# Attention and a depthwise convolution on one core: whole-array products gathered into one stretch per image

## The chip, the cores and the metric

The kernel runs on one core of a Trainium2 chip. The metric is the device time of one execution in microseconds (us). Three runs of the kernel before took 2955.26, 2948.74 and 2949.14 us, median 2949.14. One execution was also profiled; it was timed at 2951.07 us, and the span from its first to its last instruction is 2949.3 us. PE is the matrix engine, DVE the vector engine, ACT the scalar engine, POOL and SP the two engines whose queues issue most of the transfers (DMA).

## The reference

The input x is (16, 384, 32, 32) in float32: 16 images, 384 channels, 1024 pixels. Two layers follow each other, each a normalisation over 32 groups of channels, a branch, and the addition of the branch to its input:

```python
# layer 0: attention over the 1024 pixels, 8 heads of 48 channels
qkv = einsum('bnc,oc->bno', tokens(gn(x)), w_qkv)
attn = softmax(q @ k.T * 48 ** -0.5)
x = x + from_tokens(einsum('bnc,oc->bno', attn @ v, w_proj) + b_proj)
# layer 1: depthwise 7x7 convolution, the weight averaged over four rotations
x = x + dwconv(gn(x), w_sym, stride=1, pad=3)
```

The mean and variance of the first normalisation come from the input x, those of the second from the result of layer 0.

## The kernel before

**Tiles.** The 384 channels of an image are three tiles of 128 partitions by 1024 pixels, named by k (or o, for outputs). Heads are taken in four windows per image; a window has 16 key blocks of 64 keys, so an image has 64 steps (`PER_B`), and the kernel has 1024.

**Products on PE.** Two kinds alternate. The whole-array products use all 128 rows and columns of PE: q and k (`qk_step`, line 445, three pieces t = 0, 1, 2 of two products each; the fourth tile of q and k is gathered by six transfers in `qk_rest`, line 461), v (`v_step`, line 471, four products) and the projection (`proj_step`, line 597, three). The tiled products address PE as four tiles of 48 or 64 rows by 64 columns: the scores S of a step (`s_step`, line 516) and the product of their exponentials with v (`av_step`, line 536, called AV here). Each float32 product is two passes, so a step has 8 matmuls for S and 8 for AV.

**PSUM.** All whole-array products and all S share one pool of three buffers (tag "s"). ACT empties them: a copy of 128x1024 for each qk product (line 452), four small copies for each v product (line 491), the bias for a projection (line 605), and the exponential of an S into one of eight buffers (line 524).

**What else ACT does, in its one queue.** It normalises the next image's x (`x_apply`, three instructions at line 367, which wait for the load of x, line 164), squares the result of layer 0 for its variance (`x1_squares`, line 288), forms the factors of the second normalisation (`x1_groups`, lines 306 to 308, with two table loads), and applies them (`x1_chains`, line 367 again, which wait for the factors brought by the transfer at line 281).

**DVE.** It runs the convolution as taps (line 683): 49 per tile, 147 per image, in turn over the three tiles of one image, with the softmax work between them: reciprocals of the sums (line 566) and the divide (line 578), each of which waits for a small transfer on SP. Of the last two images some tiles and rows go to PE and ACT instead.

**What sets the order.** There is no scheduler at run time. The kernel is written out by a planner in Python (line 898 on), and the order of its instructions on each engine is fixed then; real time enters through the waits alone. The planner keeps two clocks, `clock` for PE and `vclock` for DVE, advanced by fixed costs (`US_STEP` and so on). `after(wait, cost, f)` puts work for DVE on a list with a due time; `catch_up(to)` writes out what is due, or taps, until `vclock` reaches `to`. Work for ACT goes into the list `applies`, in order, each with a due time and a cost; `act_slot(free)` writes out those that are due and cost no more than `free`. It is called between steps (with 4.3) and ahead of each qk product (with 9.0). A due time is thus a place in an engine's queue. If what it waits for is late, all that stands behind it in that queue waits too.

**Where the whole-array products stand.** `chunks` holds the three qk pieces of each image. `other` writes one out after every 8 steps if it is due: the pieces 0 and 1 of an image at 32 and 16 steps before the image begins, piece 2 at 16 steps into it. The v products follow the image's first 8 S. The projection of the former image follows when its last divide is done and 7 us have passed, between two steps. So an image breaks its steps five times. `scores` runs S ahead of AV by `LOOK` + 1 = 5 steps, across the border between two images. x has a single buffer: the next image is loaded (`begin_x`) once piece 2 is written.

Of the kernel before, what the change touches and what calls it, by code (L numbers as in the profile page):

```python
# [45 lines left out]
def kernel(  # L46
# [27 lines left out]
    B, C, H, W = x.shape  # L74
    N = H * W
    NK = C // P
    D = C // HEADS
    NP = HEADS // 2
    NT = N // P
# [32 lines left out]
    def run(general):  # L112
        tag = "g" if general else "f"
        with ExitStack() as stack:
# [25 lines left out]
            xds, shs, pss, mats, psums = {}, {}, {}, {}, {}  # L140
# [49 lines left out]
            v = wpool.tile([P, NT, VG] if general else [P, 2 * NT, VW], F32, name="v")  # L190
# [307 lines left out]
            def place(n):  # L498

                w, kb = divmod(n, 2 * NT)  # L500
                return w // NP, w % NP // 2, w % 2, kb
# [406 lines left out]

            US_STEP, US_QK, US_V, US_PROJ = 1.717, 5.3, 4.0, 5.3
            LOOK = 4
            clock, vclock, last_image, catching = 0.0, 0.0, 1e9, False
            later, count = [], 0
            chains, active = deque(), []
            NS = U * 2 * NT

            SIZES = [8] * 8
            PER_B = 2 * NT * NP

            def now():
                return vclock if catching else max(clock, vclock)
# [110 lines left out]
                catching = False  # L1033


            chunks, proj = deque(), deque()
            ready = {}
            x1_stats = {}
            pe_conv, pe_loads = deque(), deque(
# [6 lines left out]
            def issue(c):  # L1046
                nonlocal clock
                kind, b, i = c
                if kind == "qk":
                    act_slot(9.0)  # L1050
                    for s in range(2):
                        qk_step(b, i, s)
                        clock += US_QK
                        if s == 0:

                            catch_up(clock)
                            act_slot(9.0)
                    if i == NK - 1:
                        qk_rest(b)
                        if b + 1 < B:  # L1060
                            begin_x(b + 1)
                else:
                    v_step(b, i)
                    clock += US_V

# [5 lines left out]
            def project(b):  # L1071
                nonlocal clock
                for o in range(NK):
                    proj_step(b, o)
                    clock += US_PROJ
                    if b in ON_VECTOR:
                        after(8.0, 1.3, lambda o=o: x1_part(b, o))
                if b not in ON_VECTOR:
                    after(1.6, 0.2, lambda: x1_means(b))
# [15 lines left out]
            def x1_means(b):  # L1095
                st = x1_stats[b] = Stats(f"x1_{b}")
                st.bs = x1_bs[:, b % 2]
                nc.vector.scalar_tensor_tensor(
                    st.bs[:, :, 1::3],
                    psums.pop(b).unsqueeze(2).to_broadcast([P, NK, 2]),  # L1100
                    -1.0 / N,
                    x_mean[:, b, :].unsqueeze(2).to_broadcast([P, NK, 2]),
                    ALU.mult,
                    ALU.add,
                )
                applies.append((now() + 1.0, 4.2, lambda: x1_squares(b, st)))

            def x1_squares(b, st):
                for k in range(NK):
                    st.square(x1s[b, k], k)  # L1110
                st.gather_x1()
                after(11.0, 3.3 if b == B - 2 else 0.6, lambda: x1_aggregate(b, st))
# [9 lines left out]

            def x1_groups(b, st):
                st.groups_x1()
                applies.append((clock + 6.5, 3.7, lambda: x1_chains(b, st)))

            def act_slot(free, slow=1.0):
                nonlocal act_free
# [4 lines left out]
                    act_free = clock + slow * cost  # L1133
                    f()

            s_next, act_free = 0, 0.0

            def scores(to):

                nonlocal s_next, clock  # L1140
                while s_next < min(to, NS):
                    b, q, _, _ = place(s_next)
                    while chunks and chunks[0][1:] <= (b, q + 1):
                        issue(chunks.popleft())
                    s_step(s_next)
                    s_next += 1
                    clock += US_STEP / 2

            def between_steps():
                catch_up(clock)  # L1150
                if clock >= act_free:
                    act_slot(4.3, 2.3)
                if proj and proj[0][0] <= clock:
                    project(proj.popleft()[1])
                    catch_up(clock)

            def x1_chains(b, st):
                nonlocal vclock
# [38 lines left out]
            def begin_x(b):  # L1197
                load_x(b)
                if b == 1:
                    after(10.0, 3.8, lambda: x_channels(b))  # L1200
                else:
                    applies.append((now() + 7.0, 3.7, lambda: x_apply(b, None)))

            def x_channels(b):
                st = Stats(f"x_{b}")
# [38 lines left out]
                    proj.append((now() + 7.0, b))  # L1244


            for b in range(B):
                chunks.extend(("qk", b, t) for t in range(NK))


            ones = tpool.tile([P, N], F32, tag="t", name="ones_warm")[:, 0:HALF]
            nc.vector.memset(ones, 1.0)
            warm = psum("warm")
# [21 lines left out]
            conv_weights()  # L1275
            means_of(st.bs, x_mean[:, 0, :])
            ready[0] = 0.0
            issue(chunks.popleft())
            issue(chunks.popleft())
            every = [(b, k) for b in range(2, B) for k in range(NK)]  # L1280
            for n, bk in enumerate(every):
                after(2.0 * n, 0.0, lambda bk=bk: stream_in(*bk))
# [53 lines left out]
                    elif h == 1:  # L1336
                        after(6.0, 1.2, lambda: conv_on_pe_end(b, k))

            def other(done):

                catch_up(clock)
                if chunks:
                    _, cb, t = chunks[0]
                    when = PER_B * cb + (-32, -16, 16)[t]
                    if ready.get(cb, 1e9) <= clock and done >= when:
                        issue(chunks.popleft())
                catch_up(clock)

            def first_half(b):

# [49 lines left out]
            for b, n0, size in [  # L1400
                (b, b * PER_B + sum(SIZES[:g]), SIZES[g]) for b in range(B) for g in range(len(SIZES))
            ]:
                r = n0 - b * PER_B
                if n0 == NS - PER_B:
                    last_image = clock
                if r == 0:
                    scores(n0 + 2 * LOOK)
                    for i in range(NT // 2):
                        issue(("v", b, i))
                elif r % (2 * NT) == 0:  # L1410
                    scores(n0 + LOOK + 3)
                ending = b == B - 1 and r + size == PER_B
                if ending:
                    scores(NS)
                    catch_up(clock)
                    assert not invs and not waiting
                    first_half(b)
                    loads(1)
                for n in range(n0, n0 + size):
                    scores(n + LOOK + 1)  # L1420
                    av_step(n)
                    clock += US_STEP / 2
                    between_steps()
                w = n0 // (2 * NT)
                if (n0 + size) % (2 * NT) == 0:
                    take(w)
                    finish(w)
                if ending:
                    fast_finish(b)
                else:  # L1430
                    other(n0 + size)
                if b == B - 4 and r == 32:
                    after(0.0, 2.0, check_early)
                if b == 2 and r == 40:
                    conv_prepare()
                if b == B - 1:

                    if once("mat_0", r >= 16):
                        mat = flat2(xpool.tile([P, NK, N], F32, tag="x", name="mat_0"))
                        conv_matrices(0, mat)  # L1440
                        late["w3"] = mat[:, 2 * SH * KS * CH :][:, 0:C]
                    if once("w", r >= 32 and b - 1 in x1_stats):
                        nc.sync.dma_start(wp, w4[:, 0:NK])
                        nc.sync.dma_start(late["w3"], w4[:, NK])
                    if once("mat_1", r >= 24):
                        conv_matrices(1, flat2(qkpool.tile([P, 2, N], F32, tag="qk", name="mat_1")))
                    if once("ones", r >= 32):
                        t = opool.tile([P, N], F32, tag="o", name="masks_1")
                        nc.sync.dma_start(t, masks.rearrange("p b c -> p (b c)"))
                        late["masks"] = t.rearrange("p (b c) -> p b c", c=P)  # L1450
                if b == B - 1:
                    if r >= 32 and (b, 0) not in x1s and all(c[0] > b - 2 for c in active):
                        for k in range(NK):
                            x1s[b, k] = rpool.tile([P, N], F32, tag="x1", name=f"x1_{b}_{k}")
                            nc.gpsimd.dma_start(
                                x1s[b, k], x[b, k * P : (k + 1) * P].rearrange("p h w -> p (h w)")
                            )
                if b == B - 1 and r in (32, 40, 48):
                    loads(1)
# [66 lines left out]
```

## Time and profile before

| what | us |
|---|---|
| median of three runs | 2949.14 |
| profiled execution, its own time | 2951.07 |
| profiled execution, span | 2949.3 |
| PE busy | 2893.5 (98%) |
| DVE busy | 2571.6 (87%) |
| ACT busy | 1578.0 (54%) |
| POOL busy | 262.1 (9%) |
| last AV of image 0 / 1 / 2 / 3 / 4 | 204.8 / 378.4 / 555.9 / 732.5 / 911.1 |
| last AV of image 14 / 15 | 2684.6 / 2850.8 |
| last matmul ends | 2934.6 |

A busy time is the union of an engine's instructions. Matmuls are pipelined and overlap in the records, so PE's share is near 100% even where their starts are further apart than they need be; for PE the distance from start to start is read. In a timeline the first number is the start, the second the length of a run of alike instructions, xN their number, and a bracket the idle time ahead and what ended it. The lines of an image repeat nearly alike from image to image.

### The profile page before, as it was taken

The numbers are of one execution on the slowest core, as the hardware profiler recorded it, in microseconds if no ns is written. First come the engines' busy times: TensorE is split into PE (matmuls) and PEld (weight loads), VectorE is DVE, ScalarE is ACT, GpSimd is POOL, SyncE is SP. The second block draws the span as 40 slices with busy tenths as digits, with TensorE's granted clock in tenths as the row PEclk, the third lists the DMA queues.
The fourth block names the chain that finished last, engine by engine and source line by source line (L and its number), as shares of the span: only waits on it lengthen the run. The fifth ranks groups of instructions, "written<-read, shape, count | busy, mean of one in ns | idle before, by whom it ended". The sixth has DMA issues, their size and how long they took to land. (4 is left out here: it accounts for less than half of the span.)

```text
span 2949.3 us, 46854 instructions
## 1 busy us (share of the span) xinstructions
PE 2893.5 (98%) x19638; PEld 1132.1 (38%) x19638; DVE 2571.6 (87%) x2562; ACT 1578.0 (54%) x1873; POOL 262.1 (9%) x411
## 2 busy tenths in 40 slices
PE   9999999999999999999999999999999999999998
PEld 4333343433434343343433434343343433434333
DVE  5412998989899898998999899898998999899989
ACT  3546555465555655455465555655455465554731
POOL 2211002110100101000010100101000010100201
PEclk9999999999999999999999999999999999999999
DMA  6433012130312203012130302203012030312447
GB/s 254 150 33 64 19 33 76 25 80 19 75 27 42 69 20 85 18 33 69 27 78 19 85 18 42 70 21 83 19 33 69 21 84 18 66 37 40 97 104 178
DMA packets 77485, 176.86 MB, mean 60 GB/s; under 512 B 32096, under 2 KB 34032, under 8 KB 75728
## 3 DMA queue, kind: packets, MB, share of 16 engines
q0 software_dynamic: 34336, 114.90, 15.9%
q1 hardware_dynamic: 41216, 55.21, 7.9%
q10 hardware_dynamic: 1712, 3.67, 0.5%
q8 instruction: 156, 2.56, 0.4%
q14 instruction: 65, 0.53, 0.1%
HBM read 118.61 MB, written 28.72 MB: 50 GB/s over the span
## 5 line engine op out<-in xcount | busy, mean ns | idle before, releaser
L683 DVE SCALAR_TENSOR_TENSOR x<-xn,wsym,x 128x899 f32<-128x899 f32 (+9 forms) x2170 | 2362.9, 1164 | 45.2 <-ACT xn L367 41.5
L524 ACT ACTIVATE e<-ps_s 128x1024 f32<-128x1024 f32 x1024 | 1020.3, 1025 | 534.7 <-PE ps_s L516 531.5
L516 PE MATMUL ps_s<-qk 48*64 48x512 f32 x8192 | 1049.3, 594 | 34.8 <-ACT e L524 30.0
L536 PE MATMUL acc<-e,v 64*64 64x512 f32 x8192 | 1046.8, 593 | 0.0
L516 PEld LDWEIGHTS ps_s<-qk 48*64 48x64 f32 x8192 | 306.3, 133 | 627.0 <-issue 532.9
L536 PEld LDWEIGHTS acc<-e,v 64*64 64x64 f32 x8192 | 310.5, 133 | 576.4 <-issue 575.4
L445 PE MATMUL ps_qk<-x,wqk 128*128 128x512 f32 x1152 | 507.3, 597 | 0.0
L445 PEld LDWEIGHTS ps_qk<-x,wqk 128*128 128x128 f32 x1152 | 215.2, 190 | 291.0 <-issue 282.3
L452 ACT COPY qk<-ps_qk 128x1024 f32<-128x1024 f32 x96 | 96.9, 1009 | 307.9 <-PE ps_qk L445 307.9
L471 PE MATMUL ps_v<-wv,x 128*128 128x384 f32 x768 | 252.0, 488 | 0.0
L597 PE MATMUL ps_proj<-o,wp 128*128 128x512 f32 x540 | 235.8, 595 | 0.0
L612 POOL DMA_DIRECT2D x<-in_x x45 | 39.3, 874 | 1927.5 <-ACT x L605 1484.6
L491 ACT COPY v<-ps_v 64x384 f32<-64x384 f32 x256 | 121.4, 474 | 137.0 <-PE ps_v L471 134.8
L471 PEld LDWEIGHTS ps_v<-wv,x 128*128 128x128 f32 x768 | 144.6, 190 | 110.5 <-ACT e L524 13.0
L578 DVE TENSOR_TENSOR o<-o,inv 128x1024 f32<-128x1024 f32 x63 | 77.0, 1222 | 103.0 <-DMA inv<-inv 85.7
L605 ACT ACTIVATE x<-ps_proj,bp 128x1024 f32<-128x1024 f32 x45 | 50.1, 1114 | 211.5 <-PE ps_proj L597 211.5
L597 PEld LDWEIGHTS ps_proj<-o,wp 128*128 128x128 f32 x540 | 101.4, 190 | 134.2 <-issue 123.1
L566 DVE RECIPROCAL rec<-sums 128x16 f32<-128x16 f32 x63 | 15.6, 248 | 143.7 <-DMA sums<-sum 143.6
L549 ACT COPY o<-acc 128x512 f32<-128x512 f32 x128 | 68.0, 586 | 22.8 <-PE acc L536 22.8
L367 ACT ACTIVATE xn<-x,sc_x 128x1024 f32<-128x1024 f32 x47 | 54.9, 1231 | 30.4 <-DMA sc_x<-gr_x 23.2
L390 DVE BATCH_NORM_STATS2 bs_all<-xs 128x6 f32<-128x512 f32 x84 | 53.0, 682 | 17.9 <-DMA xs<-in_x 17.7
L367 ACT ACTIVATE x<-x,x_sc 128x1024 f32<-128x1024 f32 x42 | 51.8, 1240 | 30.7 <-DMA x<-in_x 30.1
(144 smaller groups left out, 626.2 us busy)
## 6 DMA issues: line engine op xcount, KB each, us to landing
x<-in_x POOLq DMA_DIRECT2D x90, 512.0 KB, 5.8
inv<-inv SPq DMA_DIRECT2D x126, 256.0 KB
out<-x POOLq DMA_DIRECT2D x45, 512.0 KB, 4.2
xs<-in_x POOLq DMA_DIRECT2D x42, 512.0 KB, 6.3
qk<-qk POOLq DMA_DIRECT2D x96, 128.0 KB, 6.0
o<-o SPq DMA_DIRECT2D x180, 32.0 KB
sh<-xd SPq DMA_DIRECT2D x32, 160.0 KB
x<-in_x SPq DMA_DIRECT2D x6, 512.0 KB
```

Of the source, the lines that this page charges most:

```text
L367: nc.scalar.activation(dst, src, AF.Identity, bias=self.sc[:, k, 1:2], scale=self.sc[:, k, 0:1],)
L445: nc.tensor.matmul(ps[:, h, :], lhsT=wqk[:, k, s, t, :], rhs=xns[b][:, k, h * HALF : (h + 1) * HALF], start=(k == 0), stop=(k == NK - 1),)
L452: nc.scalar.copy(halves(qks[u][:, s, :]), ps)
L471: nc.tensor.matmul(ps[:, j, 0:C], lhsT=xns[b][:, k, t * P : (t + 1) * P], rhs=wv[:, k, :], start=(k == 0), stop=(k == NK - 1),)
L491: nc.scalar.copy(dst[:, :, 0 : HEADS // 2 * (D + 1)].rearrange("p k (h d) -> p k h d", d=D + 1)[:, :, :, 0:D], src.rearrange("p k (h d) -> ...
L516: nc.tensor.matmul(ps[64 * c : 64 * c + 64, a, :], lhsT=qk[r, 1, 64 * kb : 64 * kb + 64], rhs=qk[r, 0, h * HALF : (h + 1) * HALF], start=True,
L524: nc.scalar.activation(es[n], ps, AF.Exp, scale=SCALE)
L536: nc.tensor.matmul(accs[a][64 * j : 64 * j + 64, :], lhsT=v[rows, kb, c : c + 64], rhs=e[rows, j, :], start=(kb == 0), stop=(kb == 2 * NT ...
L549: nc.scalar.copy(half_of(w)[:, a, :], accs.pop(a))
L578: nc.vector.tensor_tensor(o, o, invs.pop(u).rearrange("p (a n) -> p a n", a=2), ALU.mult)
L597: nc.tensor.matmul(ps[:, h, :], lhsT=wp[:, t, o * P : (o + 1) * P], rhs=os_[b, t // 2][:, t % 2, h * HALF : (h + 1) * HALF], start=(t == 0 ...
L683: nc.vector.scalar_tensor_tensor(acc, xn1s[b, k].rearrange("p (h w) -> p h w", w=W)[:, iy, ix], wsym[:, k, dy + PAD, dx + PAD : dx + PAD + 1],
```

## The change

`other` and the list `chunks` go. At the beginning of each image a new function, `whole_array`, writes out in one stretch the pieces 0 and 1 of qk, the four v products and piece 2, all of the image itself, and ahead of each of these items the projection of the former image, if its time has come. S can no longer run past the border of an image: `s_limit` holds it back until the stretch is written. Four S then stand ahead of the steps instead of eight. After the stretch, if the former image's projection is still not written, the PE clock is put forward to it.

Three due times in `applies` move: the squares after the means from 1 to 5 us, the normalisation of x after its load from 7 to 13, the application of the second factors from 6.5 to 9. ACT gets a slot ahead of each v product too, for work that costs at most 3.0. The planner's costs of whole-array products are lower by 0.12 to 0.14 us, and it goes through an image in 16 groups of 4 steps instead of 8 of 8; before the last group of the last image it writes the first half of that image's projection (`first_half`), which therefore moves from 8 to 4 steps ahead of the end.

```diff
-            US_STEP, US_QK, US_V, US_PROJ = 1.717, 5.3, 4.0, 5.3
+            US_STEP, US_QK, US_V, US_PROJ = 1.717, 5.16, 3.88, 5.16
...
-            SIZES = [8] * 8
+            SIZES = [4] * 16
...
                 else:
+                    act_slot(3.0)
                     v_step(b, i)
...
-                applies.append((now() + 1.0, 4.2, lambda: x1_squares(b, st)))
+                applies.append((now() + 5.0, 4.2, lambda: x1_squares(b, st)))
...
-                applies.append((clock + 6.5, 3.7, lambda: x1_chains(b, st)))
+                applies.append((clock + 9.0, 3.7, lambda: x1_chains(b, st)))
...
-                while s_next < min(to, NS):
-                    b, q, _, _ = place(s_next)
-                    while chunks and chunks[0][1:] <= (b, q + 1):
-                        issue(chunks.popleft())
+                while s_next < min(to, s_limit):
                     s_step(s_next)
...
                     act_slot(4.3, 2.3)
-                if proj and proj[0][0] <= clock:
-                    project(proj.popleft()[1])
-                    catch_up(clock)
...
-                    applies.append((now() + 7.0, 3.7, lambda: x_apply(b, None)))
+                    applies.append((now() + 13.0, 3.7, lambda: x_apply(b, None)))
...
-            for b in range(B):
-                chunks.extend(("qk", b, t) for t in range(NK))
...
-            def other(done):
-
-                catch_up(clock)
-                if chunks:
-                    _, cb, t = chunks[0]
-                    when = PER_B * cb + (-32, -16, 16)[t]
-                    if ready.get(cb, 1e9) <= clock and done >= when:
-                        issue(chunks.popleft())
-                catch_up(clock)
+            def whole_array(b):
+
+                nonlocal clock, s_limit
+                items = [("qk", 0), ("qk", 1), *(("v", i) for i in range(NT // 2)), ("qk", 2)]
+                for kind, i in items:
+                    if proj and proj[0][0] <= clock:
+                        project(proj.popleft()[1])
+                    issue((kind, b, i))
+                    catch_up(clock)
+                while b and ((b - 1) not in x1_stats and (b - 1) not in psums):
+                    clock = max(clock, proj[0][0] if proj else clock + 1.0)
+                    catch_up(clock)
+                    if proj and proj[0][0] <= clock:
+                        project(proj.popleft()[1])
+                s_limit = (b + 1) * PER_B
...
                 if r == 0:
-                    scores(n0 + 2 * LOOK)
-                    for i in range(NT // 2):
-                        issue(("v", b, i))
+                    whole_array(b)
+                    scores(n0 + LOOK)
...
-                    other(n0 + size)
+                    catch_up(clock)
```

More of the change, by code (lines that the diff above doesn't have):

```diff
@@ L1033, in catch_up @@
                 catching = False
-            chunks, proj = deque(), deque()
+            proj = deque()
             ready = {}
@@ L1134, in act_slot @@
                     f()
-            s_next, act_free = 0, 0.0
+            s_next, s_limit, act_free = 0, 0, 0.0
             def scores(to):
                 nonlocal s_next, clock
-                while s_next < min(to, NS):
-                    b, q, _, _ = place(s_next)
-                    while chunks and chunks[0][1:] <= (b, q + 1):
-                        issue(chunks.popleft())
+                while s_next < min(to, s_limit):
                     s_step(s_next)
@@ L1277, in run @@
             ready[0] = 0.0
-            issue(chunks.popleft())
-            issue(chunks.popleft())
             every = [(b, k) for b in range(2, B) for k in range(NK)]
@@ L1337, in conv_piece @@
                         after(6.0, 1.2, lambda: conv_on_pe_end(b, k))
-            def other(done):
-                catch_up(clock)
-                if chunks:
-                    _, cb, t = chunks[0]
-                    when = PER_B * cb + (-32, -16, 16)[t]
-                    if ready.get(cb, 1e9) <= clock and done >= when:
-                        issue(chunks.popleft())
-                catch_up(clock)
+            def whole_array(b):
[12 more added lines that the diff above has]
+                s_limit = (b + 1) * PER_B
             def first_half(b):
```

## The prediction

> **What bounds the kernel now.** I read the busy shares first, then the waits, then the timelines of one image (number 4, from 732.9 us on), then the end.
>
> ```profile
> PE 2893.5 (98%) x19638; PEld 1132.1 (38%) x19638; DVE 2571.6 (87%) x2562; ACT 1578.0 (54%) x1873; POOL 262.1 (9%) x411
> ```
> PE looks full, so it sets the time of all but the end, and a gain must come out of its spacing. Its timeline (start, length, engine, line, tiles):
>
> ```profile
> 791.20 1.04 PE L536 MATMUL acc<-e,v 64*64 64x512 f32 x8
> 792.17 10.57 PE L445 MATMUL ps_qk<-x,wqk 128*128 128x512 f32 x24
> 802.67 2.81 PE L516 MATMUL ps_s<-qk 48*64 48x512 f32 x24
> ...
> 815.62 1.04 PE L536 MATMUL acc<-e,v 64*64 64x512 f32 x8
> 819.61 1.82 PE L516 MATMUL ps_s<-qk 48*64 48x512 f32 x8 [2.95 <-ACT e L524]
> 821.18 1.95 PE L536 MATMUL acc<-e,v 64*64 64x512 f32 x8
> 822.89 1.22 PE L516 MATMUL ps_s<-qk 48*64 48x512 f32 x8
> 823.93 1.04 PE L536 MATMUL acc<-e,v 64*64 64x512 f32 x8
> ```
> Two losses show. (1) Groups of 8 tiled matmuls start 0.86 us apart. After 791.20 the next should start at 792.06; the whole-array group starts at 792.17. Its 24 matmuls are 0.4295 us apart, 10.31 us, yet the next S starts 10.50 us later. So one excursion into whole-array products costs 0.11 + 0.19 = 0.30 us; the mean over all excursions in the trace, from the starts of single matmuls, is 0.308. (2) Once per image an S waits 2 to 3 us for ACT, and here the groups after it are 1.6 and 1.7 us apart instead of 0.86. The waits, and ACT and POOL before this one:
>
> ```profile
> ACT x L367 <- DMA x<-in_x: 30.1, 23, 3.0
> PE ps_s L516 <- ACT e L524: 30.0, 14, 3.0
> ```
> ```profile
> 810.70 1.02 ACT L524 ACTIVATE e<-ps_s 128x1024 f32<-128x1024 f32 x1 [0.70 <-PE ps_s L516]
> 814.68 1.24 ACT L367 ACTIVATE x<-x,x_sc 128x1024 f32<-128x1024 f32 x1 [2.96 <-DMA x<-in_x]
> 816.17 2.48 ACT L367 ACTIVATE x<-x,x_sc 128x1024 f32<-128x1024 f32 x2 [0.25 <-DMA x<-in_x]
> 818.56 2.83 ACT L524 ACTIVATE e<-ps_s 128x1024 f32<-128x1024 f32 x3
> ```
> ```profile
> 797.71 1.66 POOL L694 DMA_DIRECT2D out<-x  x3
> 799.32 1.99 POOL L461 DMA_DIRECT2D qk<-qk  x4
> 804.08 0.96 POOL L461 DMA_DIRECT2D qk<-qk  x2 [2.77 <-ACT qk L452]
> 805.04 1.62 POOL L164 DMA_DIRECT2D x<-in_x  x3
> ```
> ACT reaches the normalisation of the next x at 811.7, 9 us after the last qk product (802.67), but the load was issued only at 805.04, behind three output stores of 512 KB, and its tiles land at about 814.6, 816.1 and by 817.4. The exps queue behind it, all three ps_s buffers stay full, PE stands. How long a block of ACT may be follows from two stretches (width, then busy time of PE, its weight loads, DVE, ACT, POOL; PE's clock):
>
> ```profile
> 774.00:791.20 17.20, 17.20 (x164) 6.15 (x160) 17.20 (x18) 14.39 (x18) 1.34 (x2) 1.00 0.17 29
> 807.90:826.50 18.60, 15.65 (x132) 5.20 (x128) 12.78 (x13) 11.09 (x11) 0.00 (x0) 0.91 0.40 111
> ```
> In the first, ACT is away from its exps twice, 3.5 us (squares, 775.2 to 778.7) and 3.3 us (table loads, 789.05 to 792.4): PE loses nothing. In the second it is away 6.9 us: 2.95 lost. So about 3.8 us are free, the rest is PE's.
>
> DVE is close behind. A set of 147 taps keeps it 165.2 us (147 at 1.083, and 6 of other work) in a period of 177.1 us, with 8.5 to 14.8 us of gaps. And DVE ends the kernel: PE's last matmuls end at 2934.6,
>
> ```profile
> 2941.61 1.22 DVE L970 TENSOR_TENSOR sums_of_taps<-sums_of_taps 128x1024 f32<-128x1024 f32 x1
> 2942.87 1.29 DVE L976 TENSOR_TENSOR x<-x,sums_of_taps 128x512 f32<-128x512 f32 x2
> ```
> after which 5.1 us of output transfer are left.
>
> **The change part by part.** The sum is against the profiled span, 2949.3 us; that execution was timed at 2951.07, the median of the runs is 2949.14, so span and median may be taken as one.
>
> **One stretch per image.** Before, an image has five excursions (three qk pieces, v, the projection): 77 and the first, which has only a way out. The built order of the changed kernel has one per image, 16: qk 0, qk 1, one v product, the projection of the former image, three v, qk 2. (Image 1's projection stands ahead of v.) 62 fewer at 0.308 is **19.1 us**. The matmuls are the same; between shapes inside a stretch I take nothing, since the records show no loss but on the edges; if each of its four seams lost 0.1 us, 6 us would go.
>
> Is the cover for evacuation gone? In the stretch ACT has 6 qk copies of 1.01, 16 v copies in 4 groups of 1.93, 3 projection copies of 1.3 and 3 squares in 3.5 us: 21 of 62 us, and no product waits even behind the squares: they start about 2 us after the last v product and end about 0.5 us after the first product of qk 2, whose copy they hold up that long while another buffer is free. [...] That bears on the row of five S groups, with no AV between, that now follows each stretch. An S takes 0.86 us, its exp 0.95 back to back and 1.02 alone. [...] The trace has such rows already (eight S around each v, four in a row before 736.4, 3.61 us long: regular); only 4 images lose 1.0 to 1.8 us there. Three buffers absorb a row of five; I take 0, and 12 as the far end.
>
> The projection waits for the last divide. Before, that divide is done at 746.4, 13.9 us after the image's last AV, and six small SP transfers follow; the projection at 754.9 did not wait. Now it comes 4 x 5.16 + 3.87 = 24.5 us after the last AV: no wait, about 5 us to spare after the transfers. The loop at the end of the stretch then does nothing.
>
> **Later due times.** These add no waiting instruction; they move ACT's work in its queue. x(b+1) is loaded after the stretch, and normalised after 10 exps: by S and AV steps that is 14.1 us after the last qk product, where it was 9. Behind it wait the exps, and behind these PE. The POOL order also changes: the three output stores stand behind the x load instead of ahead of it; ahead stand the two small statistics transfers and the six qk pieces. So issue is at about +2.3 to +3.9 us as before, and with 5.8 us to landing (median of the x rows of the page; 11.2 is the longest seen for this line) the tiles are there at +10, at worst +15. ACT then is away for 3 x 1.2 = 3.6 us, within the free 3.8. Five exps on come the table loads (3.3 us), then five exps, two copies, three exps and xn's 3.6 us: by then their factors, 7 us after the table loads in the trace, have long landed. So the waits go. What they cost: in images 1 to 14 the spacing of tiled matmuls is 51.7 us over regular: 34.9 in the waits and 16.8 in slow spacing. About 0.3 per image is in image 1 too, which has no such wait; it stays (4.2). That leaves **47.5 us**. (Image 1, 173.7 us against a mean of 177.1, says the same: without four excursions 172.5.)
>
> [...] The row above has the clock at 0.91 for 18.6 us after a wait of 2.95: 1.7 us lost. I go by the trace. Image 0 loses 5.2 us in its own way (factors of x(1) late, 3.1 us at 145 us), which no due time here touches; its load is earlier by place: **2 us**, 0 to 5.
>
> **x1_means +5, act_slot(3.0), groups of 4.** The squares now fall into the stretch, where they cost nothing; the v slot takes no work in the built order. Groups of four move the last image's first projection half behind four more AVs, 3.4 us, while it waited 4.8 for a divide: **3.4 us** on PE.
>
> **The end.** PE's last AV comes at 2850.8 - 19.1 - 47.5 - 2 - 3.4 = 2778.8. But the statistics of image b-1 now follow x(b+1)'s normalisation in ACT's queue, so its taps start about 39 us after the stretch, with about 44 of the 64 steps left, where they had 48 (802.9 in image 4). In the built DVE order 66 taps stand behind the last statistics of image 15 (line 354), before 56. That point was 25 us after the last AV; I take 24. Then 73.5 us as before and 10 taps at 1.083: 24 + 73.5 + 10.8 = 108.3 against 98.5. The end gives back **10 us**.
>
> Sum: 19.1 + 47.5 + 2 + 3.4 - 10 = 62; **2887 us**. As a check by DVE: taps of image 14 start about 37 us after the last stretch, near 2695; 175 busy, 5 of transfer and 10 to 17 of gaps give 2885 to 2892.
>
> **Rivals.**
> A, the x tiles are late again (ACT's wait on x in the trace, 30.1 us, is the size of PE's). For it: landing varied from 4.9 to 11.2 us. Against it: the stores are out of the way and there are 5 us more. All waits kept: 2887 + 47.5 = 2935; half, 2911.
> B, DVE becomes the bound: 165.2 busy in 172.6 leaves 7.4. Gaps inside a set were 3 to 7 us, besides 6 to 8 at its start that exist only because it is ahead. At 9.5 per set: 14 x 2.1 = 30, 2917.
> C, slower: DVE keeps gaps on waits for the sums and their inverses, in order with taps behind them, now that these are due in a denser period. It decides from 7.4 + 62/14 = 11.8 us inside a set; at 14 us, 2887 + 14 x 6.6 = 2979. Against it: before's gaps of that kind reach 7.
> D, nothing gained: not for the excursions, since the built order has them gone; with A and the PSUM row's 12 us together, 2947.
>
> **How the numbers follow.** 2887: 0.62, with its own range 2872 to 2902 (seams 6, image 0 3, gaps 7, the PSUM row in part). A: 0.15. B: 0.13. C: 0.06. D: 0.04. To leave out no more than two in ten: 2866 to 2932, which takes in B and most of A. Within 0.3% of before (2940 to 2958, about what a measurement can tell) lie D and the edge of C; faster 0.90, same 0.05, slower 0.05.
>
> **What would show it.** After: 16 excursions, each about 62 us long; ACT at line 367 for x waiting below 5 us in all and PE for e below 8; a spacing of 172 to 173.5 us between images; half clock only at start and end; DVE with over 8 us between PE's end and its own. Wrong if L367 still waits for in_x, if PE stands at the projection for o, or if the gap before a new set of taps is gone while the gaps at L566 and L578 have grown (then it is B).

## The result, and the profile after

The changed kernel takes 2910.2 us (median; 2909.7 to 2910.6), the kernel before 2948.9 in the same session (2946.9 to 2955.3): a ratio of 0.9865, 95% interval 0.9848 to 0.9882. The forecast was 2887, its range 2866 to 2932. The direction and the range hold; of the 62 us that the sum promised, 39 came. The profiled execution has a span of 2908.8 us. Its busy shares:

```profile
PE 2860.4 (98%) x19638; PEld 1137.1 (39%) x19638; DVE 2570.7 (88%) x2562; ACT 1573.6 (54%) x1873; POOL 252.2 (9%) x411
```
PE has the same instructions and is busy with them for 33 us less. Its timeline around the products of image 4, after the change (start, length, engine, line, tiles):

```profile
693.74 19.48 PE L445 MATMUL ps_qk<-x,wqk 128*128 128x512 f32 x45
713.05 4.03 PE L471 MATMUL ps_v<-wv,x 128*128 128x384 f32 x12
716.92 15.61 PE L597 MATMUL ps_proj<-o,wp 128*128 128x512 f32 x36
732.37 11.77 PE L471 MATMUL ps_v<-wv,x 128*128 128x384 f32 x36
743.98 10.46 PE L445 MATMUL ps_qk<-x,wqk 128*128 128x512 f32 x24
754.38 4.52 PE L516 MATMUL ps_s<-qk 48*64 48x512 f32 x40
758.72 1.04 PE L536 MATMUL acc<-e,v 64*64 64x512 f32 x8
...
791.40 1.04 PE L536 MATMUL acc<-e,v 64*64 64x512 f32 x8
792.26 1.04 PE L516 MATMUL ps_s<-qk 48*64 48x512 f32 x8
```
The whole stretch is one block with no idle time in it: qk 0 and 1, one v, the projection of image 3, three v, qk 2. The row of five S that follows costs nothing: its 40 matmuls are 4.34 us long, 0.868 each group of eight. From there on every group starts 0.86 us after the one before. ScalarE in the same image, at the places where it used to hold PE up (in brackets: the idle time before a row and what ended it; none here):

```profile
768.55 3.49 ACT L367 ACTIVATE x<-x,x_sc 128x1024 f32<-128x1024 f32 x3
...
789.36 3.53 ACT L367 ACTIVATE xn<-x,sc_x 128x1024 f32<-128x1024 f32 x3
```
The distance between the last AVs of two images is 172.3 us in every image from 1 to 14 (before: 173.7 to 179.5, mean 177.1). So over these images the forecast's mechanism is there in full. The waits of PE in the whole run (us in total, times, longest) show what is not:

```profile
PE ps_s L516 <- ACT e L524: 11.7, 2, 7.8
PE ps_proj_last L641 <- DVE o L578: 8.7, 1, 8.7
```
All three waits lie in the last image. A split of the span at two points of PE's trace, the last AV of image 0 and that of image 14, tells where the time went; most kernels of the experiments are in the table too.

| kernel (profiled span) | to the last AV of image 0 | per image, 1 to 14 | from the last AV of image 14 to the end |
|---|---|---|---|
| before (2949.3) | 204.8 | 177.1 | 264.7 |
| after (2908.8) | 175.0 | 172.3 | 321.9 |
| stretch only (2959.8) | 175.7 | 177.3 | 301.9 |
| due times only (2936.4) | 205.9 | 175.2 | 277.1 |
| stretch and factors' due time (2907.5) | 173.3 | 173.3 | 308.1 |
| three waits of image 15 removed (2880.5) | 172.0 | 172.3 | 296.6 |
| sorted list and two of the edits (2864.5) | 172.5 | 172.3 | 280.2 |

Before the change two qk pieces of the next image (10.4 us each) lie ahead of an image's last AV, so the first and third columns of kernels with and without the stretch differ by some 21 us for that reason alone. Even so the end of the changed kernel is 36 us longer than before, where the sum had allowed for 10 less 3.4. In that end stand three stops. PE's timeline and, below it, three windows (us, then busy time of PE, weight loads, DVE, ACT, POOL; the figure behind these is PE's granted clock):

```profile
2660.71 1.04 PE L536 MATMUL acc<-e,v 64*64 64x512 f32 x8
2665.64 1.99 PE L516 MATMUL ps_s<-qk 48*64 48x512 f32 x8 [3.89 <-ACT e L524]
2667.41 1.93 PE L536 MATMUL acc<-e,v 64*64 64x512 f32 x8
...
2688.89 1.98 PE L516 MATMUL ps_s<-qk 48*64 48x512 f32 x8 [7.80 <-ACT e L524]
...
2784.06 2.08 PE L641 MATMUL ps_proj_last<-o,wp 128*128 128x512 f32 x2 [8.67 <-DVE o L578]
```
```profile
845.00:865.00 20.00, 20.00 (x185) 7.35 (x178) 20.00 (x20) 9.48 (x10) 0.00 (x0) 1.00 0.15 38
2660.00:2680.00 20.00, 16.11 (x124) 4.89 (x118) 20.00 (x20) 11.36 (x11) 0.00 (x0) 0.83 0.07 27
2684.00:2704.00 20.00, 15.11 (x124) 5.06 (x128) 9.12 (x11) 13.64 (x16) 4.29 (x6) 0.83 0.44 86
```
The first window is an undisturbed one, at a granted clock of 1.00; the second and third, at 0.83, hold the first and second stop. Who is late in each of the three stops, from the timelines of ScalarE (ACT), VectorE (DVE) and SP's queue:

```profile
2661.18 3.50 ACT L367 ACTIVATE xn<-x,sc_x 128x1024 f32<-128x1024 f32 x3 [4.36 <-DMA sc_x<-gr_x]
...
2686.80 1.12 ACT L664 ACTIVATE xn<-xn,wsym 128x992 f32<-128x992 f32 x1 [10.64 <-DVE x L683]
```
```profile
2654.92 36.05 DVE L683 SCALAR_TENSOR_TENSOR x<-xn,wsym,x 128x960 f32<-128x960 f32 x34
...
2711.22 0.25 DVE L566 RECIPROCAL rec<-sums 128x16 f32<-128x16 f32 x1 [18.11 <-DMA sums<-sum]
...
2782.78 1.23 DVE L578 TENSOR_TENSOR o<-o,inv 128x1024 f32<-128x1024 f32 x1 [11.24 <-DMA inv<-inv]
```
```profile
2772.67 1.71 SPq L765 DMA_DIRECT2D sh<-xd  x4
2774.48 0.37 SPq L568 DMA_DIRECT2D inv<-rec  x1
2777.71 1.13 SPq L571 DMA_DIRECT2D inv<-inv  x2
```
- First stop: image 14's normalization (the branch of `x1_aggregate` for B-2, due "now") stands in ScalarE's queue before its factors have landed. ScalarE waits 4.4 us, PE 3.9, and PE's next three groups start 1.70 to 1.77 us apart instead of 0.86.
- Second: ScalarE's second early row product (L664) writes into a buffer of the pool that image 13's taps still read. They end near 2688; the products were planned against the start of image 14's chains, and the sets of taps now run later against PE. ScalarE waits 10.6 us, PE 7.8. Window 60's sums come late through both, and VectorE, whose queue has this reciprocal ahead of nearly all of image 14's taps, is idle for 18.1 us.
- Third: the reciprocal of window 62 is done at 2766.1, but on SP's queue a shifted copy (L765) is ahead of its transfer, waiting for a buffer of q and k that the last S still reads. VectorE then waits 11.2 us for the divide's inverse and PE's last projection 8.7 for the divide. Before the change the order was the other way, inverse first: the condition `r in (32, 40, 48)` fires after step 52 instead of 56 when groups have 4 steps.

VectorE ends the kernel as before (after which 5 us of output transfer are left):

```profile
2902.36 1.29 DVE L976 TENSOR_TENSOR x<-x,sums_of_taps 128x512 f32<-128x512 f32 x2
```
From the first tap of image 14 (2688.7) to the end it is 220.1 us: 175 busy, 5 transfer, 40.1 idle. The forecast's check had 10 to 17 idle.

### The profile page after: what moved, and what is told of

It is laid out like the page before. It is cut to its first block, busy times and chain, and to the rows that moved or that the text cites. A ratio compares the mean times of both kernels' runs of the same rounds, so it can differ in the third digit from the quotient of the medians.

```text
span 2908.8 us, 46868 instructions
## 1 busy us (share of the span) xinstructions
PE 2860.4 (98%) x19638; PEld 1137.1 (39%) x19638; DVE 2570.7 (88%) x2562; ACT 1573.6 (54%) x1873; POOL 252.2 (9%) x411
## 5 line engine op out<-in xcount | busy, mean ns | idle before, releaser
L683 DVE SCALAR_TENSOR_TENSOR x<-xn,wsym,x 128x930 f32<-128x930 f32 (+9 forms) x2170 | 2362.5, 1162 | 14.7 <-ACT xn L367 14.7
L516 PE MATMUL ps_s<-qk 48*64 48x512 f32 x8192 | 1037.8, 590 | 11.7 <-ACT e L524 11.7
L799 PE MATMUL ps_conv<-sh,mat 128*32 128x480 f32 (+3 forms) x656 | 68.0, 569 | 0.0
L367 ACT ACTIVATE xn<-x,sc_x 128x1024 f32<-128x1024 f32 x47 | 55.3, 1271 | 11.6 <-DVE sc_x L357 7.2
```

The lines of the kernel that those rows point to most:

```text
L516: nc.tensor.matmul(ps[64 * c : 64 * c + 64, a, :], lhsT=qk[r, 1, 64 * kb : 64 * kb + 64], rhs=qk[r, 0, h * HALF : (h + 1) * HALF], start=True,
L683: nc.vector.scalar_tensor_tensor(acc, xn1s[b, k].rearrange("p (h w) -> p h w", w=W)[:, iy, ix], wsym[:, k, dy + PAD, dx + PAD : dx + PAD + 1],
L799: nc.tensor.matmul(dst[CH * i : CH * (i + 1), :].rearrange("p (y x) -> p y x", x=W)[:, :, ox], lhsT=mats[k][:, i, d0 * KS + dx + PAD, :], ...
```

## The experiments

The changed kernel was timed in its own session, ahead of these sets of runs. The kernel before has a median of 2948.9 to 2956.6 us over all of them, and kernels without a repeated wait have the same period per image, 172.3 us, in each. A difference between sets is therefore good to a few microseconds only, and is read with the split of the profiled spans.

Theory T: the three stops of image 15 are what is missing, by way of VectorE's idle time. Rival R: VectorE's ten more taps behind the last statistics and its own work set the end; PE's stops are covered by it and removing them brings nothing. The first four kernels, run together (the kernel before: 2952.5), tell these apart.

**The shifted copies at their old steps.**

```
-                if b == B - 1 and r in (32, 40, 48):
+                if b == B - 1 and r in (36, 44, 52):
                     loads(1)
```


> The shifted copies of image 14 (L765) are asked for one group of four steps later each (after steps 40, 48 and 56 of the last image, as before the change), so that the third comes behind the last inverse on SP's queue. Theory T (three waits in image 15 ate the missing 23 us; this is the third): the divide L578's idle of 11.2 us on DVE falls to 1 to 4, PE's wait of 8.8 us ahead of the last projection to 1 to 5, DVE's idle of image 15 from 40.5 to some 32, end near 2902 us (2898 to 2905). Rival R (the ten more taps behind the projection and VectorE's own work set the end, PE's waits are covered): 2908 to 2911 us, the idle only moves to another place on VectorE.


Measured: 2899.3 us, ratio to before 0.9816 (0.9786 to 0.9846); 10.9 less than the changed kernel. In the profiled executions it is 9.2 less, of which 7.5 lie behind the last AV of image 14 (314.4 instead of 321.9), where alone the edit can act. The divide waits 2.95 us where it waited 11.2, and PE's wait for it is gone, as T says.

**The early products later.**

```
-                                clock + 2.0 + 7.0 * n,
+                                clock + 28.0 + 7.0 * n,
```


> The ten early row products of ScalarE (L664) are planned 26 us later each, so that image 13's taps have left their buffers. T: the wait of 10.6 us at the first L664 is gone, PE's stop of 8.0 us at 2689 with its half clock too, the reciprocal of window 60 comes some 10 us earlier and VectorE's idle of 18.1 us ahead of it falls to 6 to 10; end near 2900 us (2896 to 2904). R: 2908 to 2911 us.


Measured: 2899.9 us, ratio 0.9817 (0.9787 to 0.9847). The second stop is gone and the 18.1 us of VectorE became 1.7. Some of it comes back further on: a divide that had waited 4.6 us now waits 12.9, so the gain is 10 and not 16 (8.5 in the third column of the table).

**Image 14's normalization later.**

```
                 if b == B - 2:
                     st.groups_x1_vector()
-                    applies.append((now(), 3.7, lambda: x1_chains(b, st)))
+                    applies.append((now() + 6.0, 3.7, lambda: x1_chains(b, st)))
```


> Only image 14's normalization (L367 behind x1_aggregate) is planned 6 us later, so that its factors have landed. T: ScalarE's wait of 4.4 us for the factors is gone, PE's stop of 4.1 us at 2666 with the slow pace behind it too; but the second stop hangs on VectorE's image 13, which ends at 2688 whatever PE does, so it stays or grows by the time won: end 2904 to 2910 us. R: 2908 to 2911 us. Alone it tells the two little; it is half of the next run.


Measured: 2905.1 us, ratio 0.9838 (0.9808 to 0.9868). As expected the first stop went and the second grew, from 7.8 to 9.9 us (the third column: 5.3 less).

**All three.**


> The three edits together. T: no PE wait of over 3 us in image 15, last AV near 2780 us instead of 2797.9, VectorE's idle of image 15 near 18 us instead of 40.5, end 2884 to 2892 us, which is what the prediction said. R: 2905 to 2911 us, with VectorE's idle filled elsewhere.


Measured: 2882.4 us (2882.1 to 2882.8), ratio 0.9761 (0.9731 to 0.9791). The three single gains, 10.9, 10.3 and 5.1, make 26.3; together they give 27.7. In the third column it is 21.3 and 25.3. So together they give at least the sum, and no stop was covered by another. PE's longest waits in all of this run, and then VectorE and SP's queue around the last divide:

```profile
PE ps_proj_last L641 <- DVE o L627: 2.6, 2, 2.3
PE warm L1249 <- DVE ones_warm L1243: 1.5, 1, 1.5
```
```profile
2690.05 0.23 DVE L566 RECIPROCAL rec<-sums 128x16 f32<-128x16 f32 x1
...
2752.87 1.22 DVE L578 TENSOR_TENSOR o<-o,inv 128x1024 f32<-128x1024 f32 x1 [2.84 <-DMA inv<-inv]
```
```profile
2744.63 0.34 SPq L568 DMA_DIRECT2D inv<-rec  x1
2748.05 1.13 SPq L571 DMA_DIRECT2D inv<-inv  x2
2752.54 4.89 SPq L765 DMA_DIRECT2D sh<-xd  x8
```
The inverse goes first, all eight copies behind it; the reciprocal of window 60 no longer waits. The last AV is at 2766.9 us (2797.9 in the changed kernel). From image 14's first tap (2685.7) to the end it is 194.8 us, of which about 15 idle. R is refuted: VectorE does set the end, but it was the three stops that made it idle.

The next four, run together (before: 2956.6), take the parts of the change one by one, and try another remedy.

**The due times alone**, in the kernel before:

```
-                applies.append((now() + 1.0, 4.2, lambda: x1_squares(b, st)))
+                applies.append((now() + 5.0, 4.2, lambda: x1_squares(b, st)))
-                applies.append((clock + 6.5, 3.7, lambda: x1_chains(b, st)))
+                applies.append((clock + 9.0, 3.7, lambda: x1_chains(b, st)))
-                    applies.append((now() + 7.0, 3.7, lambda: x_apply(b, None)))
+                    applies.append((now() + 13.0, 3.7, lambda: x_apply(b, None)))
```


> The kernel before with the three later due times alone (x 13 us, squares 5 us, factors 9 us); its chunks of q, k and v stay spread over the image, its groups stay 8 steps. The prediction's sum gives the due times 47.5 us in images 1 to 14, and PE's image period goes from 177.1 to about 173.7 us; less what the end gives back. If the due times did it: 2897 to 2912 us (2949 less 47.5, plus 0 to 10 at the end), the x-waits of L367 gone. If the waits went because of the stretch and the due times only go with it (rival): 2925 to 2949 us.


Measured: 2936.2 us, ratio 0.9925 (0.9899 to 0.9951). The time lies in the rival's range, but not for the rival's reason: the waits of L367 for x went without the stretch, and PE's for e with them, but for one of 3.8 us in image 0. A new one stands in their place. PE's waits:

```profile
PE ps_proj L597 <- DMA o<-o: 17.8, 12, 2.7
PE ps_s L516 <- ACT qk L452: 5.9, 1, 5.9
```
The projection now waits for the last window's rows: the divide of image 3 is done 22.6 us after that image's last AV, before the change 13.9. Behind the longest of these waits, 2.70 us at image 3's projection, the next 13 matmuls take 7.48 us, where 13 whole-array matmuls of 128x512 took 5.74 before (at 699.66). Images 4 and 10 are 178 us long.

**The stretch alone**, in the changed kernel: the diff above in the other direction.


> The changed kernel with the three due times set back (7, 1 and 6.5 us), everything else as changed. By the prediction's sum it keeps the 62 excursions (19.1 us) and the groups, and has the waits of 34.9 us and the half clock behind them again: 2925 to 2935 us, with PE's wait for e (L516 <- L524) at 25 to 35 us. If the stretch alone removes the waits (rival): 2905 to 2915 us.


Measured: 2964.5 us, ratio 1.0029 (1.0020 to 1.0038): slower than the kernel before. ScalarE's and PE's waits:

```profile
ACT xn L367 <- DMA sc_x<-gr_x: 54.6, 15, 5.7
```
```profile
PE ps_s L516 <- ACT e L524: 51.2, 15, 5.5
```
ScalarE's wait for x itself fell to 0.3 us with the old due times: in the stretch the load (L164) is issued ahead of the output stores and lands in 6.7 us (median, in the trace of the changed kernel) where it took 8.8, and that is enough. But the factors' wait more than doubled. Before the change it was

```profile
ACT xn L367 <- DMA sc_x<-gr_x: 23.2, 14, 3.1
```
Both expectations were wrong: the stretch removes one of the two waits and enlarges the other.

**Groups of eight** in the changed kernel:

```
-            SIZES = [4] * 16
+            SIZES = [8] * 8
```


> The changed kernel with groups of 8 steps again. The prediction put the groups of 4 down as a gain of 3.4 us: then this is slower, 2912 to 2916 us. By theory T the groups of 4 lose what the third shifted copy costs ahead of the inverse (10.9 us by the run of the copies alone) and gain at most those 3.4: then this is faster, 2899 to 2907 us, with L578's wait of 11.2 us on DVE gone.


Measured: 2897.2 us, ratio 0.9795 (0.9769 to 0.9820): the groups of four cost 13 us. The third column agrees (309.3 instead of 321.9). With the copies at their old steps groups of four take 2899.3 (in the earlier set), which is not less; so the 3.4 us that the forecast put on the groups of four do not show.

**A list that is served by due time.** In the code the list of ScalarE's planned work is served from its head only, in the order of entry, so that image b's factors and normalization stand behind x(b+1). Here it is sorted; the edits of the copies and of image 14's normalization are in it too.

```
             def act_slot(free, slow=1.0):
                 nonlocal act_free
+                due = sorted(applies, key=lambda a: a[0])
+                applies.clear()
+                applies.extend(due)
```


> The version with the three waits of image 15 taken out in another way: the list of planned ScalarE work is kept sorted by due time, so that an image's factors and its normalization are not queued behind the next image's x (due 13 us); copies and image 14's factors as in the earlier edits. T, with the taps of every image beginning some 20 us earlier after the stretch: image 13's taps end near 2668 us instead of 2688, so the early products find their buffers free, taps of image 14 start near 2667 and VectorE's end falls by up to 20 us, until PE's own tail (last AV near 2767 us plus 105 to 108) sets it: 2868 to 2878 us. If the end is bound by VectorE's taps alone: near 2862; if the place of the taps changes nothing: 2882.


Measured: 2868.5 us (2866.4 to 2870.3), ratio 0.9700 (0.9674 to 0.9725): faster than both kernels, 42 us less than the changed one. ScalarE forms an image's factors (L306) 69.7 us after the last AV of the image, 86.7 in the changed kernel. PE has no wait at all behind the first image (the two rows that its list has, 1.5 and 1.0 us, belong to the start), and the taps begin earlier: 2136 of the 2191 are done before the last statistics (L354), 2125 in the run with all three edits, so that 55 stand behind; before the change it was 56. VectorE's longest waits:

```profile
DVE rec L566 <- DMA sums<-sum: 68.8, 23, 26.3
DVE x L683 <- ACT xn L367: 58.2, 14, 25.4
```
Of the 58.2 us for the tiles of its next set of taps, 25.4 stand ahead of the first set, image 0's. Ahead of most later sets it is 2.9 each; in the changed kernel it was 1.3 and before the change about 3.1.

The last four (before: 2951.6) follow what the two halves had left open.

**The stretch with the factors' due time only** (squares at 1, x at 7 us).


> The stretch with one due time alone, the factors' (clock + 9); squares at 1 and x at 7 us as before. If the waits of the stretch-only run (54.6 us for the factors, 15 times, at L367 xn) are only a due time that is 2.5 us too early: some 17 us of them stay (54.6 less 15 times 2.5), the clock recovers in most images, PE's period is about 173 to 174 us, 2920 to 2935 us. If the due time is enough by itself: no wait, 172.3 us, 2905 to 2912 us. If x and squares in front of it in the list are what set it: no change, 2955 to 2965 us.


Measured: 2911.0 us, ratio 0.9872 (0.9844 to 0.9901), the time of the whole change, and in the range that was expected for no waits at all; but the way there is another. The factors' wait is down, but not gone:

```profile
ACT xn L367 <- DMA sc_x<-gr_x: 8.7, 7, 5.2
```
The period is 173.3 us, 1.0 more than with all three, but the end is 308.1 instead of 321.9. The squares lie 54.3 us after the last AV in both kernels, so their due time moves nothing; x's normalization lies at 71.5 instead of 76.7. So x's later due time wins 14 us over fourteen images and loses 14 at the end.

**The stretch with x's due time only.**


> The stretch with x's due time alone (13 us); squares at 1 and factors at 6.5 us as before. In the stretch-only run x itself waited 0.3 us only. If x's due time acts by itself: nothing to win, 2955 to 2965 us with the 54.6 us of waits for the factors. If it acts through the list that is served from its head (x holds back the factors' work behind it): these waits fall below 15 us, PE's period is 172.3 to 173 us, 2905 to 2925 us.


Measured: 3002.5 us, ratio 1.0185 (1.0156 to 1.0215), which neither expectation had.

```profile
ACT xn L367 <- DMA sc_x<-gr_x: 48.8, 15, 5.3
```
```profile
PE ps_s L516 <- ACT e L524: 73.4, 16, 5.6
PE ps_proj_last L641 <- DVE o L578: 8.2, 1, 8.2
```
ScalarE waits nearly as long as in the stretch-only run. The factors' work has moved with x: L306 begins 10.0 us after x's normalization in both runs. PE loses 22 us more. The trace shows the place: the wait now falls on the border of two windows, where S is written three ahead. In image 4:

```profile
805.12 1.90 PE L516 MATMUL ps_s<-qk 48*64 48x512 f32 x16
811.68 1.98 PE L516 MATMUL ps_s<-qk 48*64 48x512 f32 x8 [4.67 <-ACT e L524]
```
ScalarE's wait there is 3.17 us; in the stretch-only run one of 3.14, which ends just ahead of such a row, costs PE 2.90. That the border is the cause was not tested by a run of its own.

**The due times alone, with the projection later.**

```
-                    proj.append((now() + 7.0, b))
+                    proj.append((now() + 10.5, b))
```


> The due-times-only run with the projection planned 3.5 us later (10.5 us behind the last divide instead of 7). Theory: what the due times alone did not bring (13 to 20 us instead of 47.5) went into PE's new wait of the projection for its divided rows (L597 <- DMA o<-o, 17.8 us, 12 times, with half clock behind the longest) and into the end. Then that wait falls below 4 us, the period to 173.7 us, and the time to 2910 to 2920 us. If another thing holds the period (VectorE's own): the wait moves and the time stays at 2931 to 2938 us.


Measured: 2953.8 us, ratio 1.0010 (0.9998 to 1.0022): no gain over the kernel before, and slower than either expectation. The projection's wait is gone, as the theory had it, but not its time; the factors' wait is back:

```profile
ACT xn L367 <- DMA sc_x<-gr_x: 56.0, 14, 4.7
```
So in the spread form, with these due times, whichever of the two was moved out of the way, the other stood there.

**The sorted list alone.**


> The changed kernel with the list kept sorted by due time and nothing else. Against the sorted run with the copies and image 14's factors edited too (2868.5 us) it has the wait for the divide (third copy ahead of the inverse) back. If the end is PE's tail there: 2875 to 2884 us, 6 to 11 us more plus a few of the factors' wait of image 14. If the sorting took all three waits out by itself: 2866 to 2871 us.


Measured: 2888.0 us, ratio 0.9792 (0.9764 to 0.9820), 19.5 more than with the two edits. The second stop is gone by itself (the taps of image 13 end earlier); the first and third stay, 5.1 and 8.3 us on PE. This is 4 us above the higher expectation, which had undervalued what these two cost together.

## Why the prediction was right or wrong

**One stretch, 19.1 us: right in the trace.** There are 16 excursions; an image without any wait goes from 173.7 us (image 1 before) to 172.3. Seams and the row of five S cost nothing: 4.34 us for five S, with 4.30 at the regular pace. So the 12 us at most that the forecast and its rival D had for emptying PSUM did not come; they were its author's estimate, 0.8 us a row, five times the 0.16 us by which an exp alone (1.02 us) is longer than an S (0.86). What the sum did not have: the stretch alone is slower than no change, because it is only paid out if the factors' due time goes with it.

**Later due times, 47.5 us: right in size together with the stretch, wrong in its reason.** The period is 172.3, the sum's 172.6; and image 0's wait, for which 2 us were taken, went too. So the last AV of image 14 is at 2586.9 us, some 9 earlier than by the sum. But the forecast argued from x's load, its landing and its later normalization, and said of the factors that they "have long landed", although the trace before already had 23.2 us of waits for them (the line under "The stretch alone"). It also took 5.8 us for the landing of x from two lines of code together; the load at L164 alone had a median of 8.8 before, and has 6.7 after the change. The runs have it the other way: the stretch alone takes x's waits away, the factors' due time takes away most of the waits that the stretch makes, and x's due time only moves some 14 us from the images to the end. The 47.5 and the 19.1 were also added as if each stood alone; alone, against the kernel before in the same session, they are 20 us of gain and 8 of loss.

**Waits of 2 to 3 us with the clock behind them.** To take the trace's 16.8 us beside the 34.9 was right: the period could not be 172.3 otherwise. In the trace before, a granted clock of 0.50 to 0.72 follows six stops of 2.09 to 2.95 us (last section).

**"Groups of four ... 3.4 us on PE": wrong, and the only term with the wrong sign.** They were read as the place of the first projection half only. The same loop variable decides after which step the shifted copies are asked for, and the step that moved is the one ahead of an inverse on SP's queue: a loss of 10.9 us (the copies alone; 7.5 in the split) to 13 (groups of eight), so this term is 11 to 16 us off. The forecast did not follow the moved step on SP's queue.

**The end, "gives back 10": right as a term, but not all of it.** From the last AV of image 15 to the end the forecast had 108.3 us and the changed kernel has 110.9. What it missed lies ahead of that: this AV was to come at 2778.8 and comes at 2797.9, though image 14's comes 9 us early; without the three stops it is at 2766.9. With the stops gone the kernel takes 2882.4; with the list sorted, which also brings the 11 taps back to their place, 2868.5: 14 us. The check by VectorE assumed 10 to 17 us of idle time behind image 14's first tap; it was 40.1, and about 15 without the stops. Its mistake was to take image 15 to be as free of waits as the others, where the factors of image 14 have a due time of their own that the diff does not touch, and where early products write into buffers that a later set of taps still holds. These two cost 16.8 us together (27.7 less 10.9; 17.8 in the split).

**The rivals, and luck.** A and D did not happen. B and C had VectorE as the bound over the whole run; but in images 2 to 12 it keeps 7.0 us of gaps per period, mostly 4.2 inside a set of taps and 2.8 at its start, where before it was 3 to 8 inside and 4 to 8 at the start. It was the bound in the last image alone, which no rival had. The range had been widened to 2932 for A and B, so that 2910 lies in it is in part luck: another loss of that size filled the place. Of the signs that the forecast named, two failed, both in image 15 alone: PE waited 11.7 us for e instead of under 8, and it stood 8.7 us at the last projection for o, where before it was 4.8.

## What to carry to other kernels

When every image gets shorter by a plan of due times, look at the first and last image as kernels of their own: branches with due times that the change leaves alone, and buffers whose release was never near the limit. The gains of two parts can be added only if each holds without the other. And for a number that sets the size of a loop's step, list everything that reads it.

## What the runs showed of the hardware

PE's granted clock after a short stop is less simple than the forecast's one row suggested. In the trace of the kernel before, PE stops 18 times for over 0.8 us at an S or AV. Behind six of these stops, of 2.09, 2.27, 2.32, 2.34, 2.73 and 2.95 us, the clock over the next 6 us is 0.50 to 0.72, and groups of eight start up to 1.76 us apart instead of 0.86. Behind the other twelve, of 0.86 to 2.68 us, it is 1.00. In the changed kernel's trace it is 0.50 over the 3 us behind each of the three long stops (3.89, 7.80 and 8.67 us).

From 2.08 to 2.95 us the length alone does not sort the ten stops of the kernel before. The 6 us behind four of them, of 2.68, 2.08, 2.09 and 2.34 us in this order (columns as in the windows above):

```profile
998.20:1004.20 6.00, 5.99 (x56) 2.17 (x60) 6.00 (x7) 4.75 (x5) 0.00 (x0) 1.00 0.00 0
1175.50:1181.50 6.00, 5.98 (x56) 2.19 (x60) 6.00 (x6) 4.76 (x5) 0.00 (x0) 1.00 0.01 3
1702.70:1708.70 6.00, 6.00 (x40) 2.02 (x44) 6.00 (x7) 3.67 (x4) 0.00 (x0) 0.72 0.00 0
2591.70:2597.70 6.00, 6.00 (x30) 1.75 (x34) 6.00 (x7) 3.27 (x4) 0.00 (x0) 0.50 0.01 3
```
Where the clock stays at 1.00 PE gets through 56 matmuls in these 6 us, behind the other two stops through 40 and 30. What tells the stops apart was not shown by any run. Whether they are why the kernel before, with waits of 2 to 3 us in most images, differs by 20 us from run to run (2944 to 2964 in one set), and the changed one by 1 us, was not tested.
